# A two-layer group-norm convolution: layer 1's last outer products in their own slot, and no column filtering in layer 2's last chunks

## The chip, the core and the metric

The kernel runs on one core of a Trainium2 chip. TensorE (PE) multiplies, VectorE (DVE) and ScalarE (ACT) move and combine, GpSimd (POOL) makes small copies and additions, SyncE (SP) issues most of the DMAs. The time is device microseconds of one execution.

## The reference

Eight images of 32 channels and 252 x 252 pixels pass through two layers. Each layer normalizes in groups of two channels, convolves with a 5x5 kernel in reflected borders, and adds the result to its input. What matters, cut short:

```python
def _gn(v, G=16, eps=1e-5):          # mean and variance over 2 channels x 252 x 252
    ...
    return ((g - m) / jnp.sqrt(s + eps)).reshape(v.shape)

x = x + _L0_conv_ref(_gn(x), L0_conv_weight)     # 5x5, by FFT, reflect padding
x = x + _L1_conv_ref(_gn(x), L1_conv_weight)
```

Layer 2's normalization needs sums over all of layer 1's output of the same image. So the weights of layer 2, which carry the scale, can be made only when the last rows of layer 1 are there.

## The kernel before

**Layout.** Pixels are split by parity of row and column: 4 parities x 32 channels make the 128 partitions. In this form a 5x5 convolution is a 3x3 one with 128x128 blocks. Down the rows the kernel uses a fast-convolution transform: four output rows come from six "points" (0 to 5), each a product with its own transformed weights `u[:, k]`, three matmuls wide (one for each column offset).

**Chunks and slots.** An image in a layer is cut into 8 chunks of 16 split rows; a chunk is written (image, layer, chunk), counted from 0, so layer "1" in code is the second. `order` interleaves layer 2 of an image with layer 1 of the next: (b+1, 0, c), (b, 1, c), and so on. Each chunk has a slot on TensorE. The slot of a chunk holds the 12 products of the inner points 2, 4, 1, 3 (`m24`, `pairs13` in PSUM), planned as 10.2 us. The outer points 0 and 5 follow either

- *late*: 6 products in the slot of the next chunk, into `sums05`, on top of parts that VectorE has put there (5.1 us planned), or
- *at once* (`at_once`, line 916): 6 products in the chunk's own slot, into the bank `extra`, with VectorE adding the parts afterwards (`outer`, line 732), or
- *by columns* (`by_columns`, line 918): the outer points are also transformed along the columns. Eight shorter products (`column_product`, line 661; two matmul instructions each, in fp32) take the place of the six: four into `extra` in the chunk's own slot, four into `sums05` in the next. Between the two halves of the own part ScalarE seeds one bank from the other (`seed_columns`, line 674). VectorE prepares the filtered inputs (`columns`, lines 585 to 602) and combines the results (`column_parts`, lines 753 to 755).

**The input transform.** `transform` (line 528) is VectorE's work for the next chunk: row differences (line 544), row quads (554, 555), the rows that need the next chunk's first two rows (546, 557), then points 2 and 4 (565, 569), 1 (575), 3 (572), and 0 and 5 (582).

**The chain.** `keep` (line 803) adds up layer 1's output: sums come with the writing instructions, squares from ScalarE (line 818), border copies in `reflect` (lines 823 to 834). `finish_stats` (line 381) puts six steps in the table at given times: `moments` on VectorE (325 to 331), `group_mean` on TensorE (337), `deviations` on VectorE (346 to 352), `group_var` on TensorE (358), `variance` with the root on ScalarE (364, 366), `inverse` on VectorE (372 to 378). Then ScalarE scales the weights (`scale_points`, 506) and POOL adds the identity blocks for the residual (`add_residual`, 474). `fetch_weights` (467) loads the unscaled weights on SP.

**Order.** Nothing reorders at run time. Every call goes through `at(t, ...)` into a table, which is sorted by planned time and then issued; each engine runs its instructions strictly in that order, and waits on the others by semaphores. `begin(i)` (line 926) sums the planned slots from `own` and `late` (923, 924). The seeds of the pair banks (`seed`, lines 691 and 693) stand on ScalarE: TensorE can't start points 1 and 3 without them.

**Input.** Chunks of layer 1 are loaded by SP. For some chunks only one column parity is loaded; POOL fixes the borders (145 to 151), and ScalarE makes the other parity (`even_columns`, line 156).

Of the kernel before, what the change touches and what calls it, by code (L numbers as in the profile page):

```python
# [53 lines left out]
def tile_conv_preact_x2(ctx: ExitStack, tc: tile.TileContext, x: bass.AP, w0: bass.AP, w1: bass.AP, out: bass.AP):  # L54
# [473 lines left out]
    def transform(t0: float, t1: float, b: int, l: int, c: int, free: float = -100.0, now=(0, 0, 0)):  # L528

        wi = WIN[l]  # L530
        got = {}

        def source():
            if l == 0:
                nxt = xs[b, c + 1] if c + 1 < NCH else xtail[b]
                return xs[b, c][:, :, 0:256:2], nxt[:, :, 0:256:2]
            return ytile[b, c], ytile[b, c + 1] if c + 1 < NCH else ytail[b]

        def row_pairs(j0: int = 0, j1: int = NT):
            if j0 == 0:  # L540
                got["v"] = vpool.tile([P, ROWS, wi], F32, tag="v", name=f"v_{b}_{l}_{c}")
            v, (t, nxt) = got["v"], source()
            r0, r1 = 4 * j0, min(4 * j1, ROWS - 2)
            V.tensor_sub(v[:, r0:r1], t[:, r0 + 2 : r1 + 2], t[:, r0:r1])  # L544
            if j1 == NT:
                V.tensor_sub(v[:, r1:ROWS], nxt[:, 0:2], t[:, r1:ROWS])
            got["vt"] = v.rearrange("p (t i) w -> p t i w", i=4)

        def row_quads(j0: int = 0, j1: int = NT):
            if j0 == 0:  # L550
                got["u"] = vpool.tile([P, 2, NT, wi], F32, tag="u12", name=f"u12_{b}_{l}_{c}")
            u1, u2, (t, nxt) = got["u"][:, 0], got["u"][:, 1], source()
            r0, k1 = 4 * j0, min(j1, NT - 1)
            stt(u1[:, j0:j1], t[:, r0 + 1 : 4 * j1 : 4], -4.0, t[:, r0 + 3 : 4 * j1 : 4], ALU.mult, ALU.add)
            stt(u2[:, j0:k1], t[:, r0 + 2 : 4 * k1 : 4], -4.0, t[:, r0 + 4 : 4 * k1 + 1 : 4], ALU.mult, ALU.add)
            if j1 == NT:
                stt(u2[:, k1], t[:, ROWS - 2], -4.0, nxt[:, 0], ALU.mult, ALU.add)

        def point2(j0: int = 0, j1: int = NT):
            if j0 == 0:  # L560
                t = tpool.tile([P, 2, NT, wi], F32, tag="t24", bufs=1, name=f"t24_{b}_{l}_{c}")
                if not fixed:
                    fixed.append(vpool.tile([P, 2, NT, WMAX], F32, tag="t13", name="t13"))
                ts[b, l, c] = {0: t, 1: fixed[0][:, :, :, 0:wi]}
            V.tensor_sub(ts[b, l, c][0][:, 0, j0:j1], got["u"][:, 1, j0:j1], got["u"][:, 0, j0:j1])

        def point4(j0: int = 0, j1: int = NT):
            vt = got["vt"][:, j0:j1]
            stt(ts[b, l, c][0][:, 1, j0:j1], vt[:, :, 1], -2.0, vt[:, :, 2], ALU.mult, ALU.add)

        def point3():
            stt(ts[b, l, c][1][:, 1], got["vt"][:, :, 1], 2.0, got["vt"][:, :, 2], ALU.mult, ALU.add)

        def point1():
            stt(ts[b, l, c][1][:, 0], got["u"][:, 1], norm[b, l][1][:, 1:2], got["u"][:, 0], ALU.add, ALU.add)

        def points05():
            if by_columns(b, l, c):
                t = vpool.tile([P, NT, 2, wi], F32, tag="u12", name=f"t05_{b}_{l}_{c}")
            else:  # L580
                t = tpool.tile([P, NT, 2, wi], F32, tag="t05", name=f"t05_{b}_{l}_{c}")
            stt(t, got["vt"][:, :, 0:2], -4.0, got["vt"][:, :, 2:4], ALU.mult, ALU.add)  # L582
            ts[b, l, c][2] = t

        def columns():

            t, (m, mo) = ts[b, l, c][2], evens_odds(l)
            sd = vpool.tile([P, 2, NT, 2, m], F32, tag="sdiff", name=f"sdiff_{b}_{l}_{c}")
            d = tpool.tile([P, NT, 2, 2, m], F32, tag="t05", name=f"d05_{b}_{l}_{c}")
            odd, even = t[:, :, :, 1 : 2 * m : 2], t[:, :, :, 2 : 2 * m + 1 : 2]  # L590
            V.tensor_add(sd[:, 0], odd, even)
            V.tensor_sub(sd[:, 1], even, odd)
            if m == mo:
                f = "p t e (m a) -> p (t e) a m"
                V.tensor_sub(  # L595
                    d.rearrange("p t e a m -> p (t e) a m"),
                    t[:, :, :, 0 : 2 * m].rearrange(f, a=2), t[:, :, :, 2 : 2 * m + 2].rearrange(f, a=2),
                )
            else:
                V.tensor_sub(d[:, :, :, 0], t[:, :, :, 0 : 2 * m : 2], t[:, :, :, 2 : 2 * m + 1 : 2])  # L600
                V.tensor_sub(d[:, :, :, 1, 0:mo], odd[:, :, :, 0:mo], t[:, :, :, 3 : 2 * mo + 2 : 2])
            ts[b, l, c][2] = d, sd

        if (b, l, c) == order[0]:
            at(t0 - 33.3, row_quads, 0, 2)
            at(t0 - 31, point2, 0, 2)
            for fn in (row_pairs, point4):
                at(t0, fn, 0, 2)
            for fn in (row_quads, point2, row_pairs, point4):
                at(t0 + 0.2, fn, 2, 4)  # L610
            at(t0 + 4.9, point1)
            at(t0 + 5.5, point3)
            at(t0 + 6.2, points05)
        else:
            for dt, fn in ((0, row_pairs), (2, row_quads), (3.6, point2), (4.2, point4)):
                at(t0 + dt, fn)
            at(max(t0 + 5.5, free + 7.8), point1)
            at(max(t0 + 5.6, free + (11.1 if by_columns(*now) else 10.25)), point3)
            at(t1, points05)
            if by_columns(b, l, c):  # L620
                at(t1 + 1.5, columns)


    def conv(b: int, l: int, c: int, t0: float, t1: float, t2: float = 0.0, j0: int = 0, j1: int = NT, m05=None, later: float = 10.2):
# [130 lines left out]
            V.tensor_sub(half(sums05, 1, both, no), odd, m12[:, :, :, 0:no])  # L755

        step = 2.55 * f
        for i, k in enumerate((2, 4, 1, 3)):
            for h in range(3):
                if first and i < 2:  # L760
# [3 lines left out]
                    at(t0 + step * (i + h / 3) + (0.85 if columns and i == 3 and h else 0.0), product, k, h)  # L764
        for i, k in enumerate(() if columns else (0, 5)):
            for h in range(3):
                at((t1 - 2 * step if m05 else t1 + later) + step * (i + h / 3), product, k, h)
        for e in range(2):
            t = t0 + (5.1 * f if e else 3.9 if first else 2.6 * f)
            at(t, seed, e)  # L770
# [13 lines left out]
                at(t2 + 0.05, outer_columns, i)  # L784
        elif m05:
            at(t0 + 12.9 * f, parts05)
            if (b, c) == (0, NCH - 1) or (l == 1 and nt == NT):
                at(t1 - 0.01, open_rest)
            at(t1, outer, 0)
            at(t1, outer, 1)  # L790
        else:
            at(t1 + 1.5, parts05)
            at(t2 + 0.05, outer, 0)
            at(t2 + 0.05, outer, 1)
        if nt < NT:
            store_half(t1, b, c, j0 // 2, got)
        elif l == 0:
            keep(t1, None if m05 else t2, b, c, got)
        else:
            store(t1 + 1.5 if m05 else t2 + 0.7, b, c, got)  # L800

# [1 line left out]
    def keep(t1: float, t2, b: int, c: int, got):  # L803
# [33 lines left out]
            at(t1 + (0.4 if t2 is None else 2.0), shift)  # L837
        last = c == NCH - 1
        if t2 is None:
            times = t1 + 0.5, t1 + (8.7 if last else 13.4), t1 + 6.6  # L840
        else:
            times = t1 + 13.5, t2 + (0.7 if last else 9.7), t2 + 7.8
        if (b, c) == (0, 0):
            times = t1 + 5.9, *times[1:]
        at(times[0], squares, 0, slice(0, NT), slice(1, 3))
# [67 lines left out]

    at_once = {order.index(n) for n in [(0, 0, c) for c in range(NCH)] + [(0, 1, 0), (B - 2, 1, NCH - 3)]}

    def by_columns(b: int, l: int, c: int) -> bool:
        if l == 0:
            return c < NCH - 1 and (b > 1 or (b == 1 and c > 1))  # L920
        return c == NCH - 1 and b < B - 1 or c in (1, 3, 5) and b == B - 1

    own = [5.1 if i in at_once else 1.7 if by_columns(*n) else 0.0 for i, n in enumerate(order)]
    late = [0.0 if i in at_once else 1.7 if by_columns(*n) else 5.1 for i, n in enumerate(order)]
# [1 line left out]
    def begin(i: int) -> float:  # L926

        return sum(10.2 + (own + [0.0])[j] + (late[j - 1] if j else 0.0) for j in range(i))


    chained = {order.index((b, 0, NCH - 1)) + 2 for b in range(B)}


    t0 = -100.0
# [53 lines left out]
    for i, (b, l, c) in enumerate(order):  # L988
# [9 lines left out]
        else:  # L998
            conv(b, l, c, t0, t1, t2, later=10.2 + own[i + 1])
        if i + 1 < len(order):  # L1000
            transform(t0 + (6.3 if i == 0 else 3.5 if i in chained else 2.9), t1 + 0.2, *order[i + 1], free=t0, now=(b, l, c))
            nb, nl, ncx = order[i + 1]
            k = inputs.index((nb, ncx)) + 2
            if nl == 0 and 2 < k < len(inputs):
                for part in parts(*inputs[k]):
                    at(t0 + (14.0 if nb == 0 and part[0] == ROWS else 4.0), load, *inputs[k], *part)
                    at(t1 + 0.2, borders, *inputs[k], *part)
                    if once(*inputs[k]):
                        at(t1 + (0.3 if part[0] == 0 else 8.5), even_columns, *inputs[k], *part)
        if c == 0 and any(by_columns(b, l, k) for k in range(NCH)):  # L1010
            t = begin(i - 1) if l == 0 and b > 1 else t1 if l == 0 else t0
            at(t + 5.4, halve_middle, b, l)
# [4 lines left out]
        if l == 0 and b + 1 < B:  # L1017
            wide = 1 if b == 0 else 2
            if c == 0:
                for j in range(2):  # L1020
                    at(begin(i - 1 if b > 1 else i) + 1.0, load_piece, b + 1, j)
            if c < NPIECE // 2:
                for j in range(2):
                    p = 2 * c + j
                    t = (t1 if wide == 2 and j else t0) + (8.6 + 2.5 * j if wide == 1 else 9.8)
                    at(t, piece_sums, b + 1, p)
                    if p + 2 < NPIECE:
                        at(t + 2.6, load_piece, b + 1, p + 2)
# [5 lines left out]
                    at(t0 + (9.5, 10.4, 11.3)[j], scale_points, b + 1, 0, ks)  # L1034
                    at(t0 + (10.4, 12.3, 14)[j], lambda b=b, ks=ks: add_residual(G, scaled[b + 1, 0], ks))
        if l == 0 and c == NCH - 1:
            at(t2 + 0.1, fetch_weights, b, 1)
            finish_stats(b, 1, *(t2 + t for t in (1.45 if b else 0.1, 3.41, 3.42, 6.85, 7.0, 7.6)))
            for j, ks in enumerate(pairs):
                at(t2 + (9.5, 10.4, 13.6)[j], scale_points, b, 1, ks)  # L1040
                at(t2 + (10.4, 12.4, 14.5)[j], lambda b=b, ks=ks: add_residual(G, scaled[b, 1], ks))

    with tc.manual_schedule(engines={E.PE, E.DVE, E.Activation, E.Pool, E.SP}):
        for _, _, fn, args, kw in sorted(table, key=lambda e: e[:2]):
# [33 lines left out]
```

## Time and profile before

| what | us |
|---|---|
| median of 3 runs | 1962.35 |
| lowest, highest run | 1960.58, 1964.09 |
| the profiled execution, whole | 1960.66 |
| its span, first to last instruction | 1958.9 |

| engine | busy us | instructions |
|---|---|---|
| PE matmul | 1894.1 | 5068 |
| DVE | 1749.5 | 2924 |
| ACT | 1400.0 | 2703 |
| POOL | 235.9 | 541 |

The mean granted TensorE clock is 0.988 of full speed. In a row of a timeline the columns are: start and length in us, engine, line, operation, output<-inputs, shape, count, and in brackets the idle time before it with what ended that wait. Busy time of a matmul overlaps with the next one, so the distance from start to start is what a matmul takes from TensorE.

### The profile page before, as it was taken

To read this page: it belongs to the slowest core of one execution; us is meant where nothing else is said; L and a number is where in the kernel's file an instruction comes from. 1 tells how busy PE (TensorE), PEld (TensorE's weight loads), DVE (VectorE), ACT (ScalarE), POOL (GpSimd) and SP (SyncE) were. 2 spreads that over 40 slices of the span, in tenths; PEclk is the share of its full clock that TensorE was granted. 3 is DMA by queue.
4 is the path that set the end of the run, shared out by engine and by line. 5 is a ranking of instruction groups with operands and counts; after the bars stand their busy time and mean duration, and the time that the engine had idled before them with its cause. 6 is when DMAs were issued, how large, how long until landed. Compare 5 with 4: busy or idle time off the path is not lost.

```text
span 1958.9 us, 19376 instructions
## 1 busy us (share of the span) xinstructions
PE 1894.1 (97%) x5068; PEld 947.7 (48%) x5068; DVE 1749.5 (89%) x2924; ACT 1400.0 (71%) x2703; POOL 235.9 (12%) x541
## 2 busy tenths in 40 slices
PE   5999999999999999999999999999999999999998
PEld 4444444444544444544544444444454445444445
DVE  7978899899989999989989999989989999988896
ACT  5866677777777777777777687776877765665575
POOL 3542000110001100011000210002000020000100
PEclk8999999999999999999999999999999999999999
DMA  9875465757765766756856757666767636541133
GB/s 271 202 163 148 107 156 141 160 125 171 163 142 126 167 157 146 168 122 151 182 131 141 168 120 182 138 144 149 149 161 165 139 88 124 113 100 50 41 78 89
DMA packets 220974, 276.09 MB, mean 141 GB/s; under 512 B 16448, under 2 KB 204224, under 8 KB 218688
## 3 DMA queue, kind: packets, MB, share of 16 engines
q1 hardware_dynamic: 220384, 272.09, 61.5%
q10 hardware_dynamic: 480, 2.77, 0.4%
q8 instruction: 40, 0.66, 0.2%
q14 instruction: 70, 0.57, 0.1%
HBM read 207.41 MB, written 67.39 MB: 140 GB/s over the span
## 4 chain that ended last, share of the span: by engine, by line
PE 87%; DVE 5%; ACT 3%; DMA 3%; POOL 1%; issue 1%; SPq 0%; ACTq 0%; POOLq 0%; DVEq 0%
PE pairs L648 31%; PE m L648 30%; PE sums L648 15%; PE sums L670 5%; PE extra L670 5%; PE extra L648 2%; DMA st<-in_x_dram 1%; DVE v L544 1%; POOL u L474 1%; DMA xs<-in_x_dram 1%; ACT junk L818 1%; DMA wraw<-in_L_conv_weight_dram 0%; ACT y L734 0%; DVE d L595 0%; ACT u L506 0%
## 5 line engine op out<-in xcount | busy, mean ns | idle before, releaser
L648 PE MATMUL pairs<-t,u 128*128 128x504 f32 (+2 forms) x1548 | 690.5, 587 | 7.9 <-ACT pairs L691 4.5
L648 PE MATMUL m<-t,u 128*128 128x508 f32 (+3 forms) x1560 | 679.2, 583 | 5.0 <-POOL u L474 2.5
L648 PEld LDWEIGHTS pairs<-t,u 128*128 128x128 f32 x1548 | 291.4, 190 | 341.6 <-issue 322.9
L648 PEld LDWEIGHTS m<-t,u 128*128 128x128 f32 x1560 | 294.5, 190 | 330.3 <-issue 315.3
L875 ACT COPY o<-y 64x508 f32<-64x508 f32 x496 | 326.6, 659 | 9.4 <-DVE y L732 1.0
L648 PE MATMUL sums<-t,u 128*128 128x508 f32 (+3 forms) x732 | 314.8, 577 | 0.0
L734 ACT ACTIVATE y<-sums 128x508 f32<-128x508 f32 (+2 forms) x120 | 64.6, 583 | 218.7 <-PE sums L648 218.7
L582 DVE SCALAR_TENSOR_TENSOR t<-v 128x1024 f32<-128x1024 f32 (+1 forms) x128 | 157.8, 1233 | 60.8 <-PE sums L648 60.1
L648 PEld LDWEIGHTS sums<-t,u 128*128 128x128 f32 x732 | 137.8, 189 | 146.0 <-issue 139.0
L710 DVE SCALAR_TENSOR_TENSOR sd<-sd,pairs 128x504 f32<-128x504 f32 (+2 forms) x258 | 166.8, 672 | 43.1 <-PE pairs L648 41.2
L145 POOL COPY xs<-xs 64x32 f32<-64x32 f32 (+3 forms) x74 | 38.7, 523 | 1115.9 <-DMA xs<-in_x_dram 811.2
L699 ACT COPY sd<-m 128x504 f32<-128x504 f32 (+2 forms) x258 | 149.9, 581 | 1.5
L818 ACT ACTIVATE junk<-y,negk 128x1008 bf16<-128x1008 f32 x144 | 148.3, 1030 | 2.5
L706 ACT COPY sd<-pairs 128x504 f32<-128x504 f32 (+1 forms) x129 | 74.1, 574 | 88.2 <-PE pairs L648 84.2
L670 PE MATMUL extra<-sdiff,wc 128*128 128x252 f32 (+2 forms) x456 | 115.6, 375 | 20.8 <-ACT extra L674 20.8
L544 DVE TENSOR_TENSOR v<-xs 128x1792 f32<-128x1792 f32 (+1 forms) x65 | 129.9, 1999 | 0.7
L544 DVE TENSOR_TENSOR v<-y 128x1806 f32<-128x1806 f32 x64 | 130.0, 2031 | 0.0
L693 ACT COPY pairs<-m 128x504 f32<-128x504 f32 (+1 forms) x129 | 72.8, 564 | 75.0 <-PE m L648 73.3
L670 PEld LDWEIGHTS extra<-sdiff,wc 128*128 128x128 f32 x456 | 85.5, 190 | 82.3 <-issue 48.4
L234 ACT ACTIVATE st<-st,negk 128x1134 f32<-128x1134 f32 x98 | 121.7, 1242 | 3.3
L228 ACT ACTIVATE st<-st 128x1134 f32<-128x1134 f32 x98 | 112.0, 1143 | 4.4 <-DMA st<-in_x_dram 3.3
L670 PE MATMUL sums<-d,u 128*128 128x252 f32 (+2 forms) x456 | 108.4, 380 | 0.0
(172 smaller groups left out, 2221.9 us busy)
## 6 DMA issues: line engine op xcount, KB each, us to landing
xs<-in_x_dram SPq DMA_DIRECT2D x176, 504.0 KB, 8.5
st<-in_x_dram SPq DMA_DIRECT2D x111, 567.0 KB, 4.4
out_dram<-o SPq DMA_DIRECT2D x488, 126.0 KB, 6.7
u<-ud SPq DMA_DIRECT2D x15, 1152.0 KB, 6.1
xs<-in_x_dram SPq DMA_DIRECT2D x30, 441.0 KB, 6.8
xs<-in_x_dram SPq DMA_DIRECT2D x28, 472.5 KB, 8.3
ud<-uraw ACTq DMA_DIRECT2D x2, 1152.0 KB, 7.5
xtail<-in_x_dram SPq DMA_DIRECT2D x64, 31.5 KB, 6.4
```

What stands on the lines that cost most here:

```text
L228: A.activation(junk, src, AF.Identity, accum_out=acc[:, 0, i : i + 1])
L234: A.activation(junk, src, AF.Square, bias=negk, accum_out=acc[:, 1, i : i + 1])
L544: V.tensor_sub(v[:, r0:r1], t[:, r0 + 2 : r1 + 2], t[:, r0:r1])
L582: stt(t, got["vt"][:, :, 0:2], -4.0, got["vt"][:, :, 2:4], ALU.mult, ALU.add)
L648: T.matmul(dst, u[:, k, 2 - i, :], rhs[:, j0 + i0 : j0 + i1, i : i + wo], start=(i == 0 and not add), stop=(i == 2), skip_group_check=add,)
L670: T.matmul(dst[:, 0, use], w, rhs[:, use], start=(i == 2), stop=True, skip_group_check=(i != 2))
L693: A.copy(dst, src)
L699: A.copy(got["sd"][:, 1 + e], m24[e][:, 0:n])
L706: A.copy(got["sd"][:, 0], pairs13[0][:, 0:n])
L710: stt(d, d, -2.0, pairs13[e][:, 0:n], ALU.mult, ALU.add)
L818: A.activation(dst, src, AF.Square, bias=negk, accum_out=acc[:, 1, at_ : at_ + 1])
L875: copy(got["o", h][halves[s], 0:m, cp::2], got["y"][halves[cp], r : r + m, :])
```

## The change

It does these things:

- The last chunk of layer 1 of *every* image is at once (before: image 0's alone). `te`, six planned steps of products after the slot's start, is the time of its outer rows; before, own outer products stood at the end of the slot, behind or among those of the previous chunk, and now they stand ahead of these.
- The chain for layer 2 starts from `te` in that slot, one slot ahead, with new planned times; so do the weight fetch, the scaling and the residual. The squares and the `reflect` copies of the last chunk get new times.
- `by_columns` no longer takes layer 2's last chunk (images 0 to 6).
- In `transform` the rows that need the next chunk form a step of their own, `last_rows`, behind the other row steps; the first chunk's second half runs row pairs ahead of point 2.
- `even_columns` of the first images is planned at 5.25 or 13.55 us into the slot (before 0.3 and 8.5, image 0's second parts still 8.5), and the first two pieces of the next image's statistics and their loads are moved.

```diff
@@ transform
-            if j1 == NT:
-                V.tensor_sub(v[:, r1:ROWS], nxt[:, 0:2], t[:, r1:ROWS])
...
-            if j1 == NT:
-                stt(u2[:, k1], t[:, ROWS - 2], -4.0, nxt[:, 0], ALU.mult, ALU.add)
+
+        def last_rows():
+
+            v, u2, (t, nxt) = got["v"], got["u"][:, 1], source()
+            V.tensor_sub(v[:, ROWS - 2 : ROWS], nxt[:, 0:2], t[:, ROWS - 2 : ROWS])
+            stt(u2[:, NT - 1], t[:, ROWS - 2], -4.0, nxt[:, 0], ALU.mult, ALU.add)
...
-            for fn in (row_quads, point2, row_pairs, point4):
-                at(t0 + 0.2, fn, 2, 4)
+            at(t0 + 0.2, row_quads, 2, 4)
+            at(t0 + 0.2, row_pairs, 2, 4)
+            at(t0 + 0.2, last_rows)
+            at(t0 + 0.2, point2, 2, 4)
+            at(t0 + 0.2, point4, 2, 4)
...
-            for dt, fn in ((0, row_pairs), (2, row_quads), (3.6, point2), (4.2, point4)):
+            for dt, fn in ((0, row_pairs), (2, row_quads), (3.2, last_rows), (3.6, point2), (4.2, point4)):
@@ conv
+        te = t0 + 6 * step if nt == NT else t1
...
-                at((t1 - 2 * step if m05 else t1 + later) + step * (i + h / 3), product, k, h)
+                at((te - 2 * step if m05 else t1 + later) + step * (i + h / 3), product, k, h)
...
-            if (b, c) == (0, NCH - 1) or (l == 1 and nt == NT):
-                at(t1 - 0.01, open_rest)
-            at(t1, outer, 0)
-            at(t1, outer, 1)
+            if c == NCH - 1 if l == 0 else nt == NT:
+                at(te - 0.01, open_rest)
+            at(te, outer, 0)
+            at(te, outer, 1)
...
-            keep(t1, None if m05 else t2, b, c, got)
+            keep(te if m05 else t1, None if m05 else t2, b, c, got)
@@ keep
-            times = t1 + 0.5, t1 + (8.7 if last else 13.4), t1 + 6.6
+            times = (t1 - 1.9, t1 + 1.6, t1 + 22) if last else (t1 + 0.5, t1 + 13.4, t1 + 6.6)
@@ the plan
-    at_once = {order.index(n) for n in [(0, 0, c) for c in range(NCH)] + [(0, 1, 0), (B - 2, 1, NCH - 3)]}
+    at_once = {order.index(n) for n in [(0, 0, c) for c in range(NCH)] + [(b, 0, NCH - 1) for b in range(B)] + [(0, 1, 0), (B - 2, 1, NCH - 3)]}
...
-        return c == NCH - 1 and b < B - 1 or c in (1, 3, 5) and b == B - 1
+        return c in (1, 3, 5) and b == B - 1
...
-                        at(t1 + (0.3 if part[0] == 0 else 8.5), even_columns, *inputs[k], *part)
+                        kb, kc = inputs[k]
+                        t = 5.25 if part[0] == 0 and (kb, kc) != (1, 0) else 13.55 if kb else 8.5
+                        at(t1 + t, even_columns, *inputs[k], *part)
...
-                    t = (t1 if wide == 2 and j else t0) + (8.6 + 2.5 * j if wide == 1 else 9.8)
+                    t = (t1 if wide == 2 and j else t0) + (8.6 + 2.5 * j if wide == 1 else 14.5 if (b, p) == (1, 0) else 9.8)
...
-            at(t2 + 0.1, fetch_weights, b, 1)
-            finish_stats(b, 1, *(t2 + t for t in (1.45 if b else 0.1, 3.41, 3.42, 6.85, 7.0, 7.6)))
+            te = t0 + 15.3
+            at(te + 0.1, fetch_weights, b, 1)
+            finish_stats(b, 1, *(te + t for t in (3.0 if b < B - 1 else 4.4, 6.85, 6.86, 10.25 if b else 9.9, 12.82, 13.55)))
             for j, ks in enumerate(pairs):
-                at(t2 + (9.5, 10.4, 13.6)[j], scale_points, b, 1, ks)
-                at(t2 + (10.4, 12.4, 14.5)[j], lambda b=b, ks=ks: add_residual(G, scaled[b, 1], ks))
+                at(te + (14.5, 15.5, 21)[j], scale_points, b, 1, ks)
+                at(te + (15.5, 17.5, 22)[j], lambda b=b, ks=ks: add_residual(G, scaled[b, 1], ks))
```

More of the change, by code (lines that the diff above doesn't have):

```diff
@@ L839, in keep @@
         if t2 is None:
-            times = t1 + 0.5, t1 + (8.7 if last else 13.4), t1 + 6.6
+            times = (t1 - 1.9, t1 + 1.6, t1 + 22) if last else (t1 + 0.5, t1 + 13.4, t1 + 6.6)
         else:
-            times = t1 + 13.5, t2 + (0.7 if last else 9.7), t2 + 7.8
+            times = t1 + 13.5, t2 + (0.7 if b == B - 1 and c == NCH - 2 else 9.7), t2 + 7.8
         if (b, c) == (0, 0):
@@ L928, in begin @@
         return sum(10.2 + (own + [0.0])[j] + (late[j - 1] if j else 0.0) for j in range(i))
-    chained = {order.index((b, 0, NCH - 1)) + 2 for b in range(B)}
     t0 = -100.0
@@ L1000, in tile_conv_preact_x2 @@
         if i + 1 < len(order):
-            transform(t0 + (6.3 if i == 0 else 3.5 if i in chained else 2.9), t1 + 0.2, *order[i + 1], free=t0, now=(b, l, c))
+            transform(t0 + (6.3 if i == 0 else 2.9), t1 + 0.2, *order[i + 1], free=t0, now=(b, l, c))
             nb, nl, ncx = order[i + 1]
@@ L1020, in tile_conv_preact_x2 @@
                 for j in range(2):
-                    at(begin(i - 1 if b > 1 else i) + 1.0, load_piece, b + 1, j)
+                    at(begin(i - 1) + 1.0 if b > 1 else t0 + (8.0 if b else 1.0), load_piece, b + 1, j)
             if c < NPIECE // 2:
```

## The prediction

> **What bounds the kernel now.** I read the page first, then the waits of the whole run, then the timeline around each place where TensorE stops.
>
> ```profile
> PE 1894.1 (97%) x5068; PEld 947.7 (48%) x5068; DVE 1749.5 (89%) x2924; ACT 1400.0 (71%) x2703; POOL 235.9 (12%) x541
> ...
> PE 87%; DVE 5%; ACT 3%; DMA 3%; POOL 1%; issue 1%; SPq 0%; ACTq 0%; POOLq 0%; DVEq 0%
> ```
>
> TensorE is the bound, and VectorE stands close behind it. A busy TensorE is not a TensorE at its pace, so I measured pace by starts: 12 matmuls of 508 columns start 5.11 us apart (246.48 to 251.59), 0.426 each; 504 columns 0.423, 378 0.317, 252 to 256 0.215, 189 to 192 0.162. All 5,068 matmuls at these paces are 1863.5 us of the 1958.9. The other 95 are places where one start comes late: about 29 before the first products, 9 after the last, 2.6 in the first chunk, and **51.8** in the middle. The middle is what the change can reach.
>
> ```profile
> ACT std L366 <- DVE var L364: 44.8, 16, 5.7
> ...
> PE extra L670 <- ACT extra L674: 20.8, 7, 3.0
> ```
>
> These are waits of the whole run (us, times, longest). Seven times TensorE waits 3.0 us for the ScalarE copy that seeds the column products, and ScalarE's longest wait is for one 128x1 value, the variance of layer 2's statistics. The timeline of image 2's end shows the two as one event:
>
> ```profile
> 650.81 0.22 DVE L352 SCALAR_TENSOR_TENSOR sq<-dev,nvar 128x1 f32<-128x1 f32 x1
> 650.95 2.03 DVE L544 TENSOR_TENSOR v<-y 128x1806 f32<-128x1806 f32 x1
> 651.09 0.38 PE L358 MATMUL m<-sq,avg_yy 128*128 128x1 f32 x2 [0.64 <-DVE sq L352]
> ...
> 654.70 0.20 ACT L366 ACTIVATE std<-var 128x1 f32<-128x1 f32 x1 [5.69 <-DVE var L364]
> ...
> 657.84 1.01 PE L670 MATMUL extra<-sdiff,wc 128*128 128x189 f32 x4 [2.97 <-ACT extra L674]
> ```
>
> The variance product is late by 0.64 us; VectorE has a 2 us difference and more queued ahead of the variance; ScalarE stands in line at the root for 5.69 us, with eight border copies and the seed (657.22) behind it. Start by start, the seven events (images 1 to 7) cost 5.24, 5.83, 5.82, 5.22, 5.23, 5.83 and 5.24, **38.4** in all, with the wait for POOL's residual adds and the slow clock after them. Image 0 has another cause:
>
> ```profile
> 135.43 0.42 ACT L156 COPY xs<-xs 64x256 f32<-64x256 f32 x1 [6.74 <-POOL xs L148]
> ...
> 137.71 8.21 PE L648 MATMUL pairs<-t,u 128*128 128x504 f32 x12 [3.13 <-ACT pairs L691]
> ```
>
> A column copy waits for POOL, which is busy with layer 2's weights; the seeds of the pair banks stand behind it. With the halved clock that follows it costs 6.3 us. The same at 172.48 (POOL adding residuals) costs 4.9, and image 0's chain 1.3 and 0.9: **13.4**.
>
> **The change part by part.**
>
> *Column filtering dropped in seven chunks.* Per chunk it removes 16 matmuls: 8 into `extra` (two groups of 4 at 0.76, as at 398.42 and 400.88) and 8 into `sums` (4 x 0.215 + 4 x 0.162), 3.03 us. It adds 6 of 508 columns (2.56) and 6 of 381 (0.320 each, between the 378 and 504 rows; 1.92): 4.48. That is +1.45, plus a bank-opening product of 0.14 (166.08 to 166.22) now once per image: 7 x 1.59 = **+11.1 us**, all on the bounding engine. VectorE loses about 4 us of filter work per image, ScalarE the seed that waited.
>
> *Outer products in their own slot, chain a slot ahead, images 1 to 6.* I walked the built order from the first product of (3,0,7) as 0, with the durations of the rows at 610 to 660. TensorE: inner products with two statistics products to 10.8, its own outer products to 15.3, those of the chunk before to 20.4, then m2 of (2,1,7) to 23.0 and the mean product. VectorE writes the outer rows by 16.8, ScalarE's squares end at 18, the moments at 18.7: 4 us before the mean product asks. The price is on VectorE: it waits in order for the mean (23.4), and the whole transform of (4,0,0) stands behind: 2 us of row pairs and five more operations give t24 at 29.2, wanted at 31.1. The variance follows at 29.3, just as ScalarE has copied pair 1; the root waits nothing. rstd 32.2, two weight scalings to 34.0, the seed 34.6 for a bank wanted at 36.2. sdiff 38.95, wanted at 39.6; column seed 41.3, wanted at 42.0. POOL's first adds end near 36, wanted at 47; its second group stands behind the borders of xs(4,2), whose load lands near 41, so 44, wanted at 52. On SP the weight fetch now stands ahead of two statistics loads and xs(4,2); it waits for products that end when it is issued. So every wait has cover, the thinnest 0.6 us. Gain 33.2; I leave 0.3 per image for the thin ones: **-31.4**.
>
> *The thin cover against a rule.* The row: with POOL's four adds running (658.82, 2.31 us), one VectorE operation took 0.81 instead of 0.69, so 0.12 us for such a group. The Trainium skill, SBUF — State Buffer, "two separate sides", speaks against moving these adds: VectorE with two SBUF inputs and GpSimd take one port pair exclusively for a whole instruction, and the other blocks. By the row the cover holds; by the rule VectorE could lose the whole 2.31 us, 1.7 beyond the cover, +10 us over six images. I take the row, which is this pair of operations itself.
>
> *Image 7.* Here the root (30.85) stands ahead of a pair seed, and then the scaling waits for rstd (33.2) with the second seed behind it: done 36.1, wanted 34.7. 1.4 us remain of 5.24: **-3.8**.
>
> *Image 0.* The moved column copies stand behind both seeds: 6.3 and 4.9 go. But between m2's evacuation and the pair-3 seed of (1,0,1) ScalarE now has the root, a 1.8 us column copy, a scaling (0.85) and statistics of a piece (2.73). From te (start of (1,0,0)): variance 15.75, after the evacuation's parts on VectorE; copy to 18.4; rstd 18.6; scaling to 19.5; statistics to 22.3; seed 22.9. TensorE wants it at 18.2: a **new wait of 4.7 us**. What is late next is the load of that piece, behind a 504 KB load on SP: 0 to 3 more. Then the clock: the row at 171 to 178 shows 3.3 us idle, then 0.5 for 3.4 us, so 1.7 lost. The rule in TensorE: Matmul & The Clock Gate ("Part 1") asks for an idle window of about 3.4 us, free-running. Here four of the seven 3.0 us gaps also fell to 0.5: by the rule those would have cost 5.24 each (36.7 in all), by the rows 38.4; I use the rows. I take 7.5 for image 0 (between 3 and 11): **-5.9**.
>
> *The rest.* In the first chunk row pairs now run ahead of point 2's second half: ready at 40.0, wanted about 40.2; nothing, within 0.3 either way. Row order in `last_rows`, thinner `halve_middle`/`column_weights` for layer 2 (only image 7 keeps them): VectorE and ScalarE work off the path, hidden by TensorE's 15 us slots.
>
> **Sum:** +11.1 - 31.4 - 3.8 - 5.9 = **-30.0 us**. Against the profiled execution's 1960.66 (span 1958.9 and 1.8 around it) 1930.7; the runs' median is 1.7 above that execution, so I forecast **1932**.
>
> **Rivals.**
> 1. *A seed still stands behind the chain* in images 1 to 6, as in 7: thin covers and ScalarE's strict order speak for it, the walk against. At 2.7 us each, +16: 1948. Chance 0.14 (1940 to 1956).
> 2. *Image 0's pile-up doesn't form* and all covers hold: ScalarE would have to reach the statistics early; the built order speaks against. 1923. Chance 0.10.
> 3. *Slower:* VectorE's wait for the mean, with the next chunk's whole transform behind it. If the mean comes late, 10 us of operations shift, and t24, sdiff and both seeds fail together. The other parts sum to +1.4, while images 1 to 6 give 33.2 less their new stalls; so it decides from a stall of 5.9 us per image (33.2 + 3.9 - 1.4 over 6), the mean 6.5 later than in the walk. At 8 us per image: 1962.4 + 1.4 - 33.2 + 48 = 1979. For it: VectorE is 96% busy in the slot before (15.31 of 15.94). Against: the squares have 4 us of cover. Chance 0.09.
> 4. *Within 0.2%* (3.9 us, what a measurement can tell from no change): stalls of 5 us return. Chance 0.04.
> 5. *It doesn't do what it says:* the built order shows the outer products ahead of the previous chunk's and the chain a slot earlier, so no chance is given.
>
> The forecast's own case has 0.63, from 1926 to 1940. The range must hold 0.8: it takes rival 2 in and half of rival 1: **1921 to 1947**. Faster by over 0.2%: 0.63 + 0.14 + 0.10 = 0.87; same 0.04; slower 0.09.
>
> **What would show it.** Right: TensorE's matmuls of 252 columns and less fall by 112, 84 more of 381 and 508; no wait of PE extra for the seed at images' ends; ACT std's longest wait near 3 us and only in images 0 and 7; image 0's first two stalls gone, one new stall of 4 to 7 us in front of pair 3 near 178. Wrong: PE pairs waiting for ACT in every image (rival 1), or VectorE's `mean` row with a wait above 5 us followed by a late t24 (rival 3).

## The result and the profile after

| | us |
|---|---|
| before, median of 4 runs beside it | 1961.46 (1960.41 to 1964.09) |
| after, median of 4 runs | 1934.31 (1933.69 to 1934.78) |
| ratio, 95% interval | 0.9859 (0.9842 to 0.9876) |
| span of the profiled execution, before and after | 1958.9, 1931.9 |

The change takes 27.0 us off the span. First the engines and the chain of work that ended last, from the page of the changed kernel:

```profile
PE 1893.9 (98%) x5054; PEld 942.2 (49%) x5054; DVE 1719.6 (89%) x2882; ACT 1390.2 (72%) x2661; POOL 238.2 (12%) x541
...
PE 94%; DMA 2%; DVE 2%; ACT 1%; issue 0%; SPq 0%; POOL 0%; ACTq 0%; DVEq 0%; POOLq 0%
```

Busy TensorE hardly moved, though it does more work; what moved is the chain, from 87% to 94% on TensorE. Then the waits of the whole run (us, times, longest):

```profile
DVE mean L346 <- PE m L337: 20.9, 6, 3.5
...
ACT std L366 <- DVE var L364: 11.1, 10, 6.0
...
PE pairs L653 <- ACT pairs L698: 7.0, 1, 7.0
...
PE m L653 <- DVE var L364: 3.0, 1, 3.0
```

The seven 3.0 us waits of the column products for their seed are gone. VectorE now waits 3.5 us for the mean in each of images 1 to 6, which by itself costs nothing: TensorE does not stop there. Two waits of TensorE are new, each once: 7.0 us for the seed of pair 3, and 3.0 us for VectorE's read of a variance. The rest is read by starts, as in the prediction. All 5,054 matmuls at their pace are 1874.7 us, where it was 1863.5. What comes on top, by place:

| place | late starts before | after | change | predicted |
|---|---|---|---|---|
| TensorE's work | 1863.5 (work) | 1874.7 (work) | +11.2 | +11.1 |
| images 1 to 6 | 34.4 | 2.3 | -32.1 | -31.4 |
| image 7 | 5.2 | 3.2 | -2.0 | -3.8 |
| image 0 | 13.5 | 10.3 | -3.2 | -5.9 |
| start and first chunk (100 us) | 31.0 | 30.3 | -0.7 | 0 |
| sum | | | -26.8 | -30.0 |

The timeline at image 2's end, where the chain ran late before (columns: start, length, engine, line, operation, count, and in brackets the idle time before it):

```profile
625.72 0.28 PE L337 MATMUL m<-mv,avg_yy 128*128 128x1 f32 x2
...
626.03 0.16 DVE L346 COPY mean<-m 128x1 f32<-128x1 f32 x1 [3.50 <-PE m L337]
...
626.95 2.03 DVE L544 TENSOR_TENSOR v<-xs 128x1792 f32<-128x1792 f32 x1 [0.18 <-issue]
...
631.29 0.69 DVE L571 SCALAR_TENSOR_TENSOR t<-v 128x512 f32<-128x512 f32 x1
...
632.14 0.20 ACT L366 ACTIVATE std<-var 128x1 f32<-128x1 f32 x1
...
633.83 5.23 PE L653 MATMUL m<-t,u 128*128 128x504 f32 x12
...
636.58 0.64 ACT L696 ACTIVATE pairs<-m,means 128x504 f32<-128x504 f32 x1
```

The root has no idle time before it, where it had 5.69. The next chunk's point 4 is ready at 632.0, and TensorE takes up that chunk at 633.8. With the first own product at 602.6 as zero, the walk of the prediction can be laid beside it: mean 23.4 (walked 23.4), point 4 ready 29.4 (29.2), root 29.5 (after 29.3), rstd 32.3 (32.2), the seed's end 34.6 (34.6). One later step of the walk came out short, the column seed:

```profile
644.26 0.58 ACT L679 ACTIVATE extra<-extra 128x504 f32<-128x504 f32 x1
...
644.89 1.01 PE L675 MATMUL extra<-sdiff,wc 128*128 128x189 f32 x4
```

It ends at 42.2 on the same scale, where 41.3 was walked and 42.0 wanted, and TensorE starts the column products behind it 0.3 us late.

Image 0's new wait:

```profile
175.68 1.83 ACT L156 COPY xs<-xs 64x1792 f32<-64x1792 f32 x1
...
177.77 0.94 ACT L506 ACTIVATE u<-u,rstd 128x768 f32<-128x768 f32 x1 [0.27 <-DVE rstd L378]
...
181.27 1.15 ACT L228 ACTIVATE st<-st 128x1134 f32<-128x1134 f32 x1 [2.56 <-DMA st<-in_x_dram]
...
184.02 0.57 ACT L698 COPY pairs<-m 128x504 f32<-128x504 f32 x1
...
184.64 2.05 PE L653 MATMUL pairs<-t,u 128*128 128x504 f32 x2 [6.99 <-ACT pairs L698]
```

This is the line that the prediction named, copy, scaling, statistics, seed, with a wait for the load of 2.56 us in it. Behind the gap seven matmuls run at half pace, most of them 0.42 us late each: 3.1 us lost.

Image 7's wait is not where the prediction put it:

```profile
1780.87 0.28 PE L358 MATMUL m<-sq,avg_yy 128*128 128x1 f32 x2
...
1781.94 1.87 PE L653 MATMUL m<-t,u 128*128 128x508 f32 x4
...
1786.55 0.15 DVE L364 TENSOR_SCALAR var<-m 128x1 f32<-128x1 f32 x1
...
1786.76 3.67 PE L653 MATMUL m<-t,u 128*128 128x508 f32 x8 [2.95 <-DVE var L364]
```

The variance lies in column 511 of the bank `m2`. Two of the next chunk's three `m2` products are ordered ahead of VectorE's read, the third behind it, and the read stands behind seven operations of VectorE's queue (points 1, 3, 0 and 5 of that chunk's transform, two differences, two inner rows): 5.4 us from the variance product's end to the read. The Trainium skill, PSUM — Partial Sum Buffer, section "PSUM bank collisions raise a hardware error", says to guard PSUM by bank and partition quadrant, or more simply by bank, and not by address, so disjoint columns don't help. No run here shows a collision; the trace shows what such a guard costs when its reader is late, 3.0 us.

### The profile page after: what moved, and what is told of

Same layout as the page of the kernel before. It is cut to its first block, busy times and chain, and to the rows that moved or that the text cites. A ratio compares the mean times of both kernels' runs of the same rounds, so it can differ in the third digit from the quotient of the medians.

```text
span 1931.9 us, 19268 instructions
## 1 busy us (share of the span) xinstructions
PE 1893.9 (98%) x5054; PEld 942.2 (49%) x5054; DVE 1719.6 (89%) x2882; ACT 1390.2 (72%) x2661; POOL 238.2 (12%) x541
## 4 chain that ended last, share of the span: by engine, by line
PE 94%; DMA 2%; DVE 2%; ACT 1%; issue 0%; SPq 0%; POOL 0%; ACTq 0%; DVEq 0%; POOLq 0%
PE pairs L653 33%; PE m L653 33%; PE sums L653 16%; PE extra L675 4%; PE sums L675 4%; PE extra L653 4%; DMA st<-in_x_dram 1%; DMA xs<-in_x_dram 0%; DVE v L544 0%; ACT junk L824 0%; DMA wraw<-in_L_conv_weight_dram 0%; DVE sd L715 0%; DVE bn L273 0%; DMA out_dram<-o 0%; DVE t L584 0%
## 5 line engine op out<-in xcount | busy, mean ns | idle before, releaser
L715 DVE SCALAR_TENSOR_TENSOR sd<-sd,pairs 128x504 f32<-128x504 f32 (+2 forms) x258 | 166.7, 670 | 47.9 <-PE pairs L653 44.7
L824 ACT ACTIVATE junk<-y,negk 128x1008 bf16<-128x1008 f32 (+1 forms) x144 | 148.2, 1029 | 8.8 <-DVE y L724 5.7
L474 POOL TENSOR_TENSOR u<-u,resid 32x64 f32<-32x64 f32 x180 | 83.9, 466 | 199.5 <-ACT u L506 188.7
L567 DVE TENSOR_TENSOR t<-u 128x512 f32<-128x512 f32 (+2 forms) x129 | 89.7, 695 | 17.2 <-PE m L653 4.1
L675 PE MATMUL extra<-sdiff,wc 128*128 128x252 f32 (+1 forms) x400 | 100.8, 373 | 0.1
```

Of the source, the lines that this page charges most:

```text
L474: eng.tensor_add(dst, dst, resid[quad(cp, rp), ks])
L675: T.matmul(dst[:, 0, use], w, rhs[:, use], start=(i == 2), stop=True, skip_group_check=(i != 2))
L715: stt(d, d, -2.0, pairs13[e][:, 0:n], ALU.mult, ALU.add)
L824: A.activation(dst, src, AF.Square, bias=negk, accum_out=acc[:, 1, at_ : at_ + 1])
```

## The experiments

All ratios are to the kernel before, run on the same chip beside them. "Late starts" are counted as in the table above.

**Column filtering kept.** The changed kernel, with

```diff
-        return c in (1, 3, 5) and b == B - 1
+        return c == NCH - 1 and b < B - 1 or c in (1, 3, 5) and b == B - 1
```

> The changed kernel with column filtering put back into layer 2's last chunk of images 0 to 6; all else as changed. It asks what dropping the filtering was for. Theory: the drop costs its TensorE work and buys no cover, because VectorE stands idle 3.5 us before the mean in each of images 1 to 6 and the filter's differences (about 2.7 us there) fit into that wait; then about 10 us come back (7 x 1.45), no stall appears, and the time is near 1924. Rival: the filter's VectorE work ahead of the mean, or the column seed in the chain's own slot, eats the cover of 0.6 to 2 us; one stall of 1.7 us or more per image undoes the saving, 1934 or later.

Measured: 1942.87 us, ratio 0.9911 (0.9896 to 0.9926), 8.6 us above the changed kernel's median (9.2 by the spans of the two profiled executions). The rival holds. TensorE's work is 1864.5, 10.2 less as computed, but late starts in images 1 to 6 rise from 2.3 to 20.9: two of 1.15 and 1.17 us per image and smaller ones. Its waits, of the whole run:

```profile
PE m L653 <- DVE t L567: 6.9, 7, 1.0
...
DVE mean L346 <- PE m L337: 5.8, 6, 1.0
...
PE m L653 <- POOL u L474: 4.9, 5, 1.0
```

VectorE's wait for the mean shrinks from 3.5 to 1.0, so 2.5 us of filter work did fit in. But the filter is larger than the estimate: VectorE is busy 1759.2 us instead of 1719.6, 5.7 us per chunk. The other 3.2 us push what follows, and VectorE has no gap left to take them: from 636.0 to 664.0 it is busy 27.6 of 28.0 us. One wait is for point 2 of the next chunk (L567). The other is put down to POOL's residual adds, but the transform was no earlier there: at image 2's end L567 ends at 650.30, and TensorE starts at 650.41. In each of images 1 to 6 TensorE starts 0.1 us after L567's end, so this wait too is set by the transform.

**Column filtering dropped, chain late.** The kernel before, with

```diff
-        return c == NCH - 1 and b < B - 1 or c in (1, 3, 5) and b == B - 1
+        return c in (1, 3, 5) and b == B - 1
```

> The kernel before with only the column filtering of those seven chunks dropped; the chain of statistics stays where it was. Theory: the seed that waited belonged to the first chunk of the next image's layer 1, which keeps its filtering, so all seven events stay (38 us) and TensorE gets 7 x 1.45 = 10.2 us more work: about 1972. Rival: it was VectorE's filter work (some 4 us per image) that made the variance late; without it the events halve, about -9 net, near 1952.

Measured: 1962.11 us, ratio 0.9999 (0.9984 to 1.0014), between the two. TensorE gets its 10.2 us more. Of each event in images 1 to 6 the seed's wait stays, while the late variance product (0.8) and the wait for the residual adds (1.0) go; image 7's event goes altogether. Waits:

```profile
ACT std L366 <- DVE var L364: 39.3, 16, 5.1
...
PE extra L670 <- ACT extra L674: 17.8, 6, 3.0
```

So relief on VectorE (1714.5 busy instead of 1749.5) is worth something and pays for the added TensorE work, no more (the profiled execution is 3.9 us faster than the kernel's median, so its late starts are on the low side): the root still stands 5.1 us in front of a seed. The waiting seed is that of the next image's first chunk, which keeps its filtering, as the theory had it.

**Statistics behind the seed in image 0.** The changed kernel, with

```diff
-                    t = (t1 if wide == 2 and j else t0) + (8.6 + 2.5 * j if wide == 1 else 14.5 if (b, p) == (1, 0) else 9.8)
+                    t = (t1 if wide == 2 and j else t0) + (8.6 + 2.5 * j if wide == 1 else 15.6 if (b, p) == (1, 0) else 9.8)
```

> The changed kernel with one edit in image 0: the statistics of image 2's first piece (load wait 2.6 us and 2.7 us of ScalarE) stand behind the seed of pair 3 instead of ahead of it. Theory (ScalarE's order sets the stall of 7.15 us near 177): the seed ends near 179.3, wanted at 177.5, so 1.8 us of the 7.15 stay and the 3.0 us of slow clock behind it go: -8.4, near 1926. Rival: the stall is set by the late load or by the residual adds that follow on POOL, and comes back in front of the next chunk: no change, 1934.

Measured: 1932.61 us, ratio 0.9859 (0.9842 to 0.9876), no change in the ratio. The theory was right about the seed, and the rival about the return of the wait, though not about its cause. The wait of 7.15 falls to 1.75, as computed, with no slow clock behind it; and a wait comes back 14 us later in front of the next chunk. From that kernel's timeline:

```profile
187.05 1.15 ACT L228 ACTIVATE st<-st 128x1134 f32<-128x1134 f32 x1 [0.62 <-DMA st<-in_x_dram]
...
194.58 0.65 ACT L696 ACTIVATE pairs<-m,means 128x508 f32<-128x508 f32 x1
...
195.38 2.35 PE L653 MATMUL pairs<-t,u 128*128 128x508 f32 x3 [4.33 <-ACT pairs L696]
```

Between 180.6 and 189.6 ScalarE now does the statistics of three pieces, 2.6 to 2.8 us each, in front of border copies and the next seed. In the changed kernel the stall itself had given ScalarE the time for them. It is not the load that holds TensorE there: ScalarE waits 0.3 and 0.6 us for loads in that stretch. In this trace image 0 loses 8.2 us instead of 10.3; image 7, which the edit doesn't touch, loses 2.9 more to slow clock, so the span doesn't show the gain.

**The variance read earlier in image 7.** The changed kernel, with the planned time of `variance` for the last image moved:

```diff
-            finish_stats(b, 1, *(te + t for t in (3.0 if b < B - 1 else 4.4, 6.85, 6.86, 10.25 if b else 9.9, 12.82, 13.55)))
+            finish_stats(b, 1, *(te + t for t in (3.0 if b < B - 1 else 4.4, 6.85, 6.86, 10.25 if b else 9.9, 12.82 if b < B - 1 else 11.5, 13.55)))
```

> The changed kernel with one edit in image 7: VectorE reads the variance before it works off the seven operations that stood ahead of it (3.5 us earlier). Theory: TensorE's wait of 2.95 us for that read goes, but the scaling of the weights still stands ahead of pair 3's seed on ScalarE (seed done near 1791.6, wanted at 1789.6), so a stall of about 2.0 us takes its place: -1.1, near 1933. Rival: the seed is not wanted before it is there; the whole 3.1 goes and no stall is left in image 7, 1931.

Measured: 1932.16 us, ratio 0.9856 (0.9838 to 0.9874); its span is 1930.2, 1.7 less than the changed kernel's; 1.1 of that is in image 7, the rest where the edit doesn't reach, image 0's slow clock for the most part.

```profile
1782.35 0.15 DVE L364 TENSOR_SCALAR var<-m 128x1 f32<-128x1 f32 x1
...
1782.55 5.38 PE L653 MATMUL m<-t,u 128*128 128x508 f32 x12 [1.11 <-DVE var L364]
...
1790.37 0.58 ACT L698 COPY pairs<-m 128x508 f32<-128x508 f32 x1
...
1791.01 2.82 PE L653 MATMUL pairs<-t,u 128*128 128x508 f32 x6 [0.52 <-ACT pairs L698]
```

Late starts in image 7 are about 2.0 us, the theory's total, at two places instead of one: 1.27 still in front of `m2`, since the read stands behind one difference, and 0.69 in front of the seed. That the seed's own wait was hidden under the other one is shown by this run: it appears once the other is smaller.

**Image 0's part alone.** The kernel before, with the change's row order and column copies:

```diff
+        def last_rows():
...
-                        at(t1 + (0.3 if part[0] == 0 else 8.5), even_columns, *inputs[k], *part)
+                        kb, kc = inputs[k]
+                        t = 5.25 if part[0] == 0 and (kb, kc) != (1, 0) else 13.55 if kb else 8.5
+                        at(t1 + t, even_columns, *inputs[k], *part)
```

> The kernel before with image 0's part of the change alone: column copies placed behind the pair seeds, last rows apart, the first chunk's order; the chain and the column filtering stay as before. Theory: the stalls near 134 and 171 (6.3 and 4.9 us) go and nothing takes their place, because the chain is not yet a slot ahead: -11.2, near 1950, and the new wait of 7 us near 177 belongs to the chain's move. Rival: the copy of the third input chunk behind the seeds makes the wait near 177 by itself; then -11.2 + 7 to 10, near 1958.

Measured: 1951.34 us, ratio 0.9959 (0.9945 to 0.9973). The stalls near 134 and 171 are gone, and near 177 there is no wait:

```profile
175.78 0.57 ACT L698 COPY pairs<-m 128x504 f32<-128x504 f32 x1
177.94 2.78 PE L653 MATMUL pairs<-t,u 128*128 128x504 f32 x6
...
193.16 2.37 PE L653 MATMUL pairs<-t,u 128*128 128x508 f32 x5 [2.53 <-ACT pairs L696]
```

Late starts in image 0 fall from 13.5 to 3.9, so 9.6 us and not 11.2: the chain's own waits grew from 2.2 to 3.9. In images 1 to 6 they stay at 33.4, so the row order alone gives nothing there. That rules out the rival: the copy behind the seeds does not make the wait near 177 by itself. The filter is not its cause either, since the first experiment's kernel keeps the filter and has the wait (6.9 us). What remains is the chain's move, which sets root and scaling in front of that seed, and the later place of the statistics (planned at 14.5 instead of 9.8; this is moved for image 2's first piece only, while the loads are for its first two). No run parts these two fully; in the third experiment, with that piece behind the seed, 1.75 of the 7.15 us are left.

**Seeds first.** The changed kernel, with ScalarE's order mended at both places:

```diff
-                        t = 5.25 if part[0] == 0 and (kb, kc) != (1, 0) else 13.55 if kb else 8.5
+                        t = 5.25 if part[0] == 0 and (kb, kc) != (1, 0) else 15.4 if (kb, kc) == (1, 2) else 13.55 if kb else 8.5
-                    t = (t1 if wide == 2 and j else t0) + (8.6 + 2.5 * j if wide == 1 else 14.5 if (b, p) == (1, 0) else 9.8)
+                    t = (t1 if wide == 2 and j else t0) + (8.6 + 2.5 * j if wide == 1 else 18.5 if (b, p) == (1, 0) else 20.6 - 0.1 * j if b == 1 and p < 3 else 9.8)
-            finish_stats(b, 1, *(te + t for t in (3.0 if b < B - 1 else 4.4, 6.85, 6.86, 10.25 if b else 9.9, 12.82, 13.55)))
+            finish_stats(b, 1, *(te + t for t in (3.0 if b < B - 1 else 4.4, 6.85, 6.86, (9.9, *[10.25] * (B - 2), 9.4)[b], 12.82 if b < B - 1 else 9.45, 13.55)))
-                at(te + (14.5, 15.5, 21)[j], scale_points, b, 1, ks)
+                at(te + (15.5 if b == 0 else 17.2 if b == B - 1 else 14.5, 17.3 if b == B - 1 else 15.5, 21)[j], scale_points, b, 1, ks)
-                at(te + (15.5, 17.5, 22)[j], lambda b=b, ks=ks: add_residual(G, scaled[b, 1], ks))
+                at(te + (17.4 if b == B - 1 else 15.6 if b == 0 else 15.5, 17.5, 22)[j], lambda b=b, ks=ks: add_residual(G, scaled[b, 1], ks))
```

> The changed kernel with ScalarE's order mended in images 0 and 7: pair 3's seed ahead of the third input chunk's copy, of the weight scalings and of the statistics of image 2's first piece; two more statistics of that image behind the next chunk's seeds; in image 7 the variance read 5 us earlier and two scalings behind the seed. Theory: both places hold nothing but orders of ScalarE and VectorE, so 10.3 - 0.3 and 3.2 - 0.3 us go: span near 1919, about -13 from the changed kernel, time near 1921. Rival: image 0 is held by its late loads or by the residual adds on POOL, and the wait comes back in front of the next chunk as it did when only the statistics moved (5.9 us there): 1928 or more.

Measured: 1920.46 us (1920.27 to 1920.56), ratio 0.9795 (0.9775 to 0.9815), 13.9 us under the changed kernel; its span is 1918.6. At the place of the 7 us wait:

```profile
174.87 5.23 PE L653 MATMUL pairs<-t,u 128*128 128x504 f32 x12
...
175.47 0.58 ACT L698 COPY pairs<-m 128x504 f32<-128x504 f32 x1
176.07 1.84 ACT L156 COPY xs<-xs 64x1792 f32<-64x1792 f32 x1
```

The seed precedes the copy, and twelve matmuls run through. Between 170 and 1815 us late starts are 2.5 us in all (0.25 in image 0, 0.1 in image 7). Both places were orders in ScalarE's and VectorE's queues; POOL's adds were only replanned to follow the scaling that they need. The medians of this and of the changed kernel were not measured side by side; by the two ratios they lie 12.5 us apart, by the spans 13.3. What is left above TensorE's pace lies in the first 100 us (30.2) and behind the last matmul (about 9).

## Why the prediction was right

The forecast was 1932; the time is 1934.3, and the span fell by 27.0 where 30.0 were summed. The list of late starts that it began with comes to 92.4 of its 95.4 us; nothing in the sum rests on the rest.

**TensorE's work** came as counted: 112 short matmuls fewer, 84 of 381 and 508 columns and 14 bank openings more, 11.2 us.

**Images 1 to 6** came as walked, to 0.2 us for each step of the chain listed with the result. One cover did not hold: the column seed came 0.9 us later than walked, with 0.7 of cover, and costs about 0.3 us in each of images 2 to 6. That is what the 0.3 per image had been left for; it is more than half of the 2.3 us of late starts. Rival 3's long queue behind VectorE's wait for the mean did no harm: the mean came at 23.4 as walked, with VectorE idle 3.5 us before it.

**The row against the rule on the shared port.** The row's price was right: in image 7 twelve adds of POOL run for 7 us beside VectorE, and six operations of VectorE lose 0.7 us in all. But that does not speak against the rule:

```profile
1781.15 0.69 DVE L571 SCALAR_TENSOR_TENSOR t<-v 128x516 f32<-128x516 f32 x1
...
1793.05 0.70 DVE L567 TENSOR_TENSOR t<-u 128x516 f32<-128x516 f32 x1
...
1793.24 0.68 POOL L474 TENSOR_TENSOR u<-u,resid 32x64 f32<-32x64 f32 x1
...
1793.66 0.81 DVE L571 SCALAR_TENSOR_TENSOR t<-v 128x516 f32<-128x516 f32 x1
...
1795.71 0.67 DVE L715 SCALAR_TENSOR_TENSOR sd<-sd,pairs 128x508 f32<-128x508 f32 x1
...
1796.21 0.31 POOL L474 TENSOR_TENSOR u<-u,resid 32x64 f32<-32x64 f32 x1
```

An add takes 0.31 us beside L715, which reads `pairs` from PSUM, and 0.68 beside L567, which reads SBUF alone; there it ends 0.17 us after L567 does. So it is with all of this trace's 180 adds. The 102 that begin beside no VectorE operation, or beside one with an input in PSUM, take 0.31 to 0.32. Of the 78 that begin beside one with SBUF inputs only, 73 end 0.17 to 0.19 us after its end, even where that makes an add 2.07 us long; the other five begin just before it and take 0.31. POOL does wait for the whole instruction. VectorE loses little because it waits for single adds and not for a group: of its operations that begin during an add, none is over 0.13 us above its usual time. The prediction's "the whole 2.31 us" took four adds for one instruction; counted by add, row and rule agree.

**Image 7 failed in its step.** It was "the root (30.85) stands ahead of a pair seed, and then the scaling waits for rstd (33.2) with the second seed behind it", 1.4 us. The walk followed ScalarE alone. It did not ask which TensorE product comes next into the bank that holds the variance, and the late read stopped that one first, for 3.1 us. That no slow clock followed was luck (last section). It shows in a sign that the prediction gave, too: ScalarE's longest wait at the root was to be near 3 us and is 6.0, in this image. The scaling ahead of the seed was real too, 0.7 us in the fourth experiment.

**Image 0 was right in mechanism and short in size.** Of "a **new wait of 4.7 us**" with "0 to 3 more" for the load, about 1.1 was taken; the load cost 2.56, and 4.7 + 2.6 is close to the 7.15 found. The clock was put at 1.7 and cost 3.1. The total, 10.3, lies inside the 3 to 11 given.

**One term was right, but its worth was not seen.** "+11.1" stood as the price of dropping the filter, beside a gain of 31.4 from the chain. The experiments show that these two are not separable. Against the profile before, late starts in images 1 to 6, and what TensorE's work has gained in the whole run, are:

| | chain late | chain a slot ahead |
|---|---|---|
| filter kept | 34.4, +0 | 20.9, +1.0 |
| filter dropped | 27.8, +10.2 | 2.3, +11.2 |

Dropping alone gives back 6.6 in these images for 10.2 of work; moving alone gives 13.5; both together 32.1 for 11.2. The upper left figure holds 4.9 us of slow clock of that one execution, the lower left 6.0, the right column none. Without it the gains are 7.7, 8.6 and 27.2: the two parts together still give far more than their sum. The cover in the walk, "t24 of (4,0,0) at 29.2, wanted at 31.1", exists because VectorE's queue is shorter by 5 to 5.7 us per chunk, and that is what the added TensorE work buys. The prediction named the relief ("VectorE loses about 4 us of filter work per image") and gave it no price in the sum, which would make the kernel that keeps the filter the better one by 10 us; it is 8.6 us worse.

Of the rivals, neither a late mean nor seeds behind the chain in images 1 to 6 showed, beyond the 0.3 us above. Image 0's pile-up formed; it took the last experiment's edits to take it away.

## What to carry to other kernels

Where two engines are both above 95% busy in a stretch (in the changed kernel TensorE 100% and VectorE 97% from 626 to 663 us), a cheaper form for the one can be the dearer one in time: price an edit by what it does to the second engine's queue, and test two edits together as well as apart. When a chain is walked, follow each value to every reader and each buffer to its next writer, not only the queue in which the wait was seen. A stall that is taken away exposes what it covered: moving one item out of the way moved the wait by one chunk, and only setting all later work behind the seeds removed it.

## What the hardware showed that was not expected

The same gap costs different amounts of clock, and the traces show why. TensorE's wait of 2.95 us in image 7 was followed by no slow matmul in the changed kernel, and by 2.9 us of loss in the third experiment's kernel, whose edit is in image 0. Here are the two waits, cut at the places where the granted clock can change (window in us, its length, busy time and number of instructions of each engine, granted clock as PEclk, DMA share, GB/s). The first two lines are of the changed kernel, the last two of the third experiment:

```profile
1781.48:1784.89 3.41, 2.33 (x6) 0.76 (x4) 3.41 (x7) 0.00 (x0) 0.00 (x0) 1.00 0.00 0
1784.89:1788.30 3.41, 1.54 (x4) 0.83 (x5) 3.33 (x7) 0.58 (x2) 0.00 (x0) 1.00 0.00 0
...
1779.71:1783.13 3.42, 1.34 (x4) 0.28 (x2) 3.42 (x7) 0.00 (x0) 0.00 (x0) 1.00 0.00 0
1783.13:1786.54 3.41, 2.55 (x3) 1.17 (x4) 3.24 (x10) 0.65 (x2) 0.00 (x0) 0.50 0.00 0
```

In each of the eight traces of this case all changes of the clock lie on a grid of 3.413 us, whose phase differs from execution to execution. In the changed kernel the wait fell across a grid line, with 1.08 us idle before it and 1.87 after; in the third experiment 2.08 us of it fell into one step, and the next ran at half clock. Between 100 and 1900 us this holds for all 4,204 steps of the eight traces: a step at full clock with up to 1.99 us of idle TensorE was followed by full clock, and one with more by half clock (20 times; the shortest idle time with it was 1.990 us, the longest without it 1.992). A slow step was followed by another where it had 0.59 us or more idle in it.

The Trainium skill, TensorE: Matmul & The Clock Gate ("Part 1"), has such a free-running window of about 3.4 us, and the slow clock after at least one idle window. The traces agree on the window, but about 2.0 us of idle time in one was enough. A full slow step costs half of its 3.41 us, 1.7.

So, as an estimate from these figures, a gap near 3 us costs nothing more, up to 1.7 us, or with enough of it in the slow step too about 3, by where it falls; a lone gap under 2 us costs nothing more, and one over 4 us always does.

The spread of the runs fits this, though it is not shown run by run: the 13 runs of the kernel before beside the first experiment, with nine gaps near 3 us in the trace, lie 7.6 us apart, the four of the last experiment, with none, 0.3.
